# One clock for each engine to place layer one's weight sums and token sums, a tile place lent, staging banks kept

## The chip, the cores and the metric

The kernel runs on one core of one Trainium2 chip. The metric is the device time of the program in microseconds (us), as the median of several runs; the time before is 2650.01 us, with runs from 2649.26 to 2651.77. Where the trace is read, the times are those of one profiled execution of 2648.42 us.

## The reference

Two layers of attention over graphs, on 128 graphs of 64 tokens (32 x 512 x 768 in the inner function is only the shape in which the weights were first made), 768 numbers to a token, in float32. What matters:

```python
h = max(layernorm(x), 0)
for l in range(2):
    u_left  = einsum('bih,bjh->bij', h, h @ W_left[l].T)  / sqrt(768)
    u_right = einsum('bih,bjh->bij', h, h @ W_right[l].T) / sqrt(768)
    u = u_left on and above the diagonal, u_right below it
    e = exp(u) * adj
    attention = e / (e.sum(axis=2) + 1e-10)
    ctx = attention @ (h @ W_lin[l].T + b_lin[l])
    h = relu((ctx - mean) / (std + 1e-3) * ln_a[l] + ln_b[l])
out = x + h
```

The two products with `W_left` and `W_right` are 18 blocks of 256 x 256 on three thirds of the tokens' 768 numbers; the kernel computes them with fewer multiplications by a fixed bilinear scheme.

## The kernel before

Line numbers are those of the kernel before; in the kernel after, the same helper stands 8 lines lower near the top and 84 lower near the end.

**Stages.** For each layer there are a first pass (`pass_one`), which makes the scores and the attention, and a second (`pass_two`), which makes the linear part, the context and the norm. The tokens are cut into 16 batches of 512, numbered 0 to 15, and each batch into two parts of 256. A part is held transposed in a tile `ht` ([128, 6, 256], 768 KB), of which there are six places. In layer one a batch comes to its `ht` by a chain: load x, statistics on VectorE (DVE), the normalisation on ScalarE (ACT), four transposes on DVE into the tile `xb` (one place only, L465), four stores to DRAM (L461), and two loads of `ht` (L368).

**The first pass.** It counts slots, two to a product. Layer one begins with 12 plain blocks (24 matmuls each, slots 0 to 71) for parts 0 and 1; then come ten supers, k = 1 to 10, of three parts each. A super is 40 products (`PRODUCTS`, numbered 0 to 39), each of a weight form with a token form: 8 matmuls of 128 x 256 into one of the banks C, D, X, Y in turn (later also Z and V). Layer two has a super 0 in place of the plain blocks. After product 3 of a super come the scores of the super before (L733, 192 matmuls). ACT and DVE read each bank into the tiles `m` (`reads`, L910, L914, L245); a bank is used again four products later.

**Weight sums.** The weight forms are linear combinations of the 18 raw blocks: 101 sums of two values (`W_OPS`, numbered 18 to 118). Layer one computes them while it runs, in `Weights`: on DVE, or, where the first factor is 1, on GpSimd (POOL). A DVE sum may be staged: ACT first copies one operand into a PSUM bank (Z, V or one of the score banks; L517) and DVE adds from there (L522, L245). The result overwrites an operand that has no other use, or takes one of 51 places `g`. Layer two loads its forms ready made.

**Token sums.** The token forms are 38 sums (`T_OPS`, numbered 9 to 46) of the nine pieces of a super's parts; `Tokens` issues them on POOL (L245), at most 11 of them alive, in places `g`. They are given out one at a time: either ahead, by `tokens.step`, when POOL's clock allows it, or by `tokens.need`, just before the product that uses them.

**The order** is written out by hand and by these clocks; no scheduler changes it. Each engine works through its own queue in that order. `put(slot, f)` plans a step at a slot; `turn_of(slot)` runs the planned steps and then gives out weight sums and token sums, by a clock that is estimated for DVE and POOL:

```python
now = slot * 0.86 if l == 0 or slot >= 80 else slot * 0.6 + 20.8
...
while clock["vector"] <= now and weights.some(nc.vector):
    clock["vector"] += 0.62
...
if clock["pool"] <= now + 1.5 and tokens.step(slot):
    clock["pool"] = max(clock["pool"], now) + 1.35
```

The clock starts at zero in each call of `pass_one`. At the end of the last super of a layer, `final` also plans the second pass's beginnings: the 9 blocks of `W_lin` are loaded, centred on ACT (L233, L237) and combined by 17 sums (`sums_n`, in turn on POOL and DVE), and the first token sums of the second pass go to POOL. The masks `wm` (L745) are POOL's as well.

Of the kernel before, what the change touches and what calls it, by code (L numbers as in the profile page):

```python
# [17 lines left out]
def kernel(  # L18
# [55 lines left out]
            slot += step  # L74
        return slot

    def timed(us, f):
        f.vector = us
        return f

    def run(slot):
        if slot in plan:
# [303 lines left out]
    def transpose_rows(l, u, pool):  # L386

        key, xr, todo = (1, l, u), XR[l, u], []
        if l == 0:
            mv = stat.tile([P, Q, 2], F32, name="mv0", bufs=2)  # L390
            sd = stat.tile([P, Q], F32, name="sd0", bufs=2)
            rs = stat.tile([P, Q], F32, name="rs0", bufs=2)
            nb = stat.tile([P, Q], F32, name="nb0", bufs=2)

            def scale(q0, q1):
                def deviation():
                    nc.scalar.activation(sd[:, q0:q1], mv[:, q0:q1, 1], AF.Sqrt, bias=eps_in)

                def inverse():
                    nc.vector.reciprocal(rs[:, q0:q1], sd[:, q0:q1])  # L400
                    if q1 - q0 == 1:

                        nc.vector.tensor_scalar(nb[:, q0:q1], mv[:, q0:q1, 0], rs[:, q0:q1], -1.0,
                                                op0=ALU.mult, op1=ALU.mult)
                        return
                    nc.vector.scalar_tensor_tensor(nb[:, q0:q1], mv[:, q0:q1, 0], -1.0, rs[:, q0:q1],
                                                   op0=ALU.mult, op1=ALU.mult)
# [6 lines left out]
            stats = [timed(1.2, lambda q=q: mean_var(mv[:, q, :], [xr[q][:, :HH], xr[q][:, HH:]])) for q in range(Q)]  # L414
            norms = [lambda q=q: norm(q) for q in range(Q)]
            if u:
                for f in stats + [lambda: [f() for f in scale(0, Q)]] + norms:
                    todo.extend([f, None])
            else:

                dev, inv = zip(*(scale(q, q + 1) for q in range(Q)))
                todo.extend([stats[START[0]], dev[START[0]]])
                for q, after in zip(START, START[1:] + (None,)):
                    if after is not None:
                        todo.append(stats[after])
                    todo.append(inv[q])
                    if after is not None:
                        todo.append(dev[after])
                    if q == START[2]:

                        todo.append(lambda: turn(0, START[0]))
                    todo.append(norms[q])
# [29 lines left out]
                                  xb[a * 32:(a + 1) * 32].rearrange("i (c b) q j -> i c b (q j)", b=4))  # L462

        for q in range(Q):
            todo.append(timed(0.9, lambda q=q: nc.vector.transpose(  # L465
                xb[:, :, q, :], xr[q].rearrange("p (b j) -> p b j", j=32))))
            todo.append(None)
        todo.append(store)
        return todo
# [1 line left out]
    def places(pool, shapes, names):  # L471
        for n in names:
            shape, bufs = shapes[n]
            pool.tile(shape, F32, name=n, bufs=bufs)

    class Weights:
        def __init__(self, ops, plain, stay, extra=()):
            self.at, self.left, self.stay = {}, list(ops), stay  # L480
            self.uses = {}
            for _, a, _, b, _ in W_OPS:
                for v in (a, b):
                    self.uses[v] = self.uses.get(v, 0) + 1
            for v in range(18):
                self.uses[v] = self.uses.get(v, 0) + plain
            for f in FORMS:
                self.uses[f] = self.uses.get(f, 0) + 1
            self.stage = []
            self.mine = {id(t) for t in extra}  # L490
            self.extra = deque(extra)

        def used(self, v):
            self.uses[v] -= 1
# [4 lines left out]
        def take(self):  # L499
            of = max(self.extra, free, key=len)  # L500
            return of.popleft() if of else None

        def emit(self, eng, op):
            v, a, ca, b, cb = op
            x, y = self.at[a], self.at[b]
            dead = next((s for s in (a, b) if self.uses[s] == 1 and not (self.mine and s >= 18)), None)
            t = self.take() if dead is None else self.at[dead]
            if t is None:
                return False
            if dead is not None:  # L510
                self.uses[dead] = 0
                del self.at[dead]
            if self.stage and eng is nc.vector:
                bank = self.stage.pop(0)
                self.stage.append(bank)
                bank = bank.rearrange("p (c d) -> p c d", c=K2)
                nc.scalar.copy(bank, x)  # L517
                x = bank
            if ca == 1:
                added(eng, t, "+" if cb > 0 else "-", x, y)  # L520
            else:
# [6 lines left out]
            self.left.remove(op)  # L528
            return True

        def some(self, eng, reach=10):
            for op in self.left[:reach]:
                if op[1] in self.at and op[3] in self.at and (eng is nc.vector or op[2] == 1):
                    if eng is nc.vector and op[2] == 1 and any(o[2] != 1 and o[1] in self.at and o[3] in self.at
                                                               for o in self.left[:reach // 2]):
                        continue
                    return self.emit(eng, op)
            return False

        def need(self, v):  # L540
            if v not in self.at:
                op = next(o for o in self.left if o[0] == v)
                self.need(op[1])
                self.need(op[3])
                assert self.emit(nc.vector, op)
            return self.at[v]


# [34 lines left out]
    class Tokens:  # L583
        LIMIT = 11

        def __init__(self, l):
# [4 lines left out]
                self.uses[v] = self.uses.get(v, 0) + 1  # L591
            self.count = {}


        def value(self, k, v, cut=False):
            if v >= 9:
# [11 lines left out]
                    for p in SUPER[0]]  # L608

        def step(self, slot, eng=None):  # L610
            if self.k >= len(SUPER) or slot < self.ready.get(self.k, 10 ** 9) or self.out >= self.LIMIT or not free:
# [17 lines left out]
        def used(self, k, v):  # L629
            n = self.count[k, v] = self.count.get((k, v), 0) + 1  # L630
            if v >= 9 and n == self.uses[v]:
                free.append(self.at.pop((k, v)))
                self.out -= 1

        def need(self, k, v):
# [2 lines left out]
            return self.value(k, v)  # L638


    SPACE = (((0, 46, 97), (-12, 34, 97)), ((10, 46, 97), (10, 46, 97)))

    TOKENS, fetch = [Tokens(l) for l in range(L)], deque()
# [11 lines left out]
    def pass_one(l, start, final):  # L655
        with tc.tile_pool(name=f"one{l}", bufs=2, reuse_waits="tile") as sp, \
# [170 lines left out]
            if l:  # L827
                weights.uses.update({f: 1 for f in FORMS})
            weights.at = W[l, "raw"]
            clock = {"pool": 0.0, "vector": 0.0}  # L830

            def turn_of(slot):
                now = slot * 0.86 if l == 0 or slot >= 80 else slot * 0.6 + 20.8
                clock["vector"] = max(clock["vector"], now - 1.0) + sum(getattr(f, "vector", 0.0) for f in plan.get(slot, ()))
                run(slot)
                if fetch and slot >= start["weights"] and slot % 3 and free:
                    fetch.popleft()()
                if weights.left and slot >= start["weights"]:
                    while clock["vector"] <= now and weights.some(nc.vector):
                        clock["vector"] += 0.62  # L840
                    if clock["pool"] <= now and start["pool"] <= slot < start["tokens"]:
                        if weights.some(nc.gpsimd, 40):
                            clock["pool"] = max(clock["pool"], now) + 1.35
                if clock["pool"] <= now + 1.5 and tokens.step(slot):
                    clock["pool"] = max(clock["pool"], now) + 1.35


            follow = {}

            def prepare(b, slot, step=1):  # L850
# [5 lines left out]
                for t in range(2):  # L856
# [7 lines left out]
                    put(at, lambda p=p, hold=before >= 0: load_part(1, l, p, hold))  # L864
# [14 lines left out]
            for n, (w, t) in enumerate(order):  # L879
                bank = bank_of(n % CHAINS)  # L880
                for j in range(3):
# [3 lines left out]
                    if j == 2:  # L885
                        if n == 0 and mid:
                            mid()
                            weights.stage = [KEEP["Z"], KEEP["V"], KEEP["scores"][:, 0]]
                        nc.scalar.copy(into(6 * t + w), out_of(bank))
                    turn_of(slot + 1)  # L890
                    slot += 2
            weights.stage = []

            last = len(SUPER) - 1
            for k in range(FIRST_OF[l], len(SUPER)):
# [8 lines left out]
                def reads(i):  # L904
                    for o, c in READS[i]:
                        bank = out_of(bank_of(CHAINS * (k - 1) + i % CHAINS), k == 0, o)
                        to = into(o, k == 0)
                        if o not in seen:
                            seen.add(o)
                            nc.scalar.activation(to, bank, AF.Copy, scale=float(c))  # L910
# [454 lines left out]
```

## Time and profile before

| what | value |
|---|---|
| median of 3 runs | 2650.01 us (2649.26 to 2651.77) |
| profiled execution | 2648.42 us, its span 2646.6 us |
| mean granted TensorE clock | 0.995 |
| busy: PE / DVE / POOL / ACT | 98% / 67% / 67% / 35% of the span |
| DMA | 331.84 MB, 125 GB/s |

The span is counted from the first to the last instruction. A row of a timeline gives the start and the length of a group of like instructions on one engine, the line, the operation, the tiles written and read, shapes and count, and in brackets the idle time ahead of it and what ended that. A row of the busy time by stage gives a window, its length, each engine's busy time with the count of instructions, then the granted clock of TensorE (1.00 is full), the DMA engines' share and their rate.

### The profile page before, as it was taken

The page shows a single profiled execution, that of the slowest core. Times are in us where ns is not written, and L with a number is a line of the kernel's source. Part 1 is how long each engine was busy: PE and PEld are TensorE (multiplying, and loading weights), DVE is VectorE, ACT ScalarE, POOL GpSimd, SP SyncE. Part 2 cuts the span into 40 slices and gives each one's busy share as a digit, 9 for nine tenths or more (in the row PEclk, how much of TensorE's full clock was granted, in tenths as well). Part 3 has the DMA queues.
Part 4 walks back from the last instruction along what each step waited for, and adds up shares of the span by engine and source line. Part 5 has one row for each costly group of instructions (what it writes and reads, how often), then busy time and mean ns, then how long its engine had stood idle before and what let it go on. Part 6 is the DMA issues. An engine that isn't in the chain of part 4 may idle for free. (4 is left out here: it accounts for less than half of the span.)

```text
span 2646.6 us, 47202 instructions
## 1 busy us (share of the span) xinstructions
PE 2591.6 (98%) x18122; PEld 2217.1 (84%) x18122; DVE 1780.6 (67%) x2888; ACT 935.4 (35%) x1969; POOL 1763.1 (67%) x1392
## 2 busy tenths in 40 slices
PE   9899999999999999999999999999999989999998
PEld 8788888888888888888798888888888878887886
DVE  7878787777768445554456667677666676666667
ACT  5522223223113244454542222122222335555453
POOL 4766676666668657676276666667666657878786
PEclk9999999999999999999999999999999999999999
DMA  7443534343421354445794424253532215555655
GB/s 220 113 111 86 124 93 110 93 119 79 98 60 56 123 156 149 159 139 182 219 282 101 121 68 108 71 129 93 136 98 70 67 49 157 157 167 166 177 161 146
DMA packets 258465, 331.84 MB, mean 125 GB/s; under 512 B 56002, under 2 KB 190402, under 8 KB 258242
## 3 DMA queue, kind: packets, MB, share of 16 engines
q1 hardware_dynamic: 241442, 320.56, 44.3%
q10 hardware_dynamic: 16800, 8.26, 1.2%
q8 instruction: 145, 2.38, 0.4%
q14 instruction: 78, 0.64, 0.1%
HBM read 213.39 MB, written 115.34 MB: 124 GB/s over the span
## 5 line engine op out<-in xcount | busy, mean ns | idle before, releaser
L245 POOL TENSOR_TENSOR g<-ht 128x512 f32<-128x512 f32 (+1 forms) x620 | 785.9, 1279 | 420.8 <-PE Z L702 71.6
L245 POOL TENSOR_TENSOR g<-g,g 128x512 f32<-128x512 f32 (+1 forms) x310 | 397.9, 1291 | 136.7 <-PE C L702 22.0
L245 POOL TENSOR_TENSOR g<-ht,g 128x512 f32<-128x512 f32 (+1 forms) x272 | 346.1, 1282 | 164.8 <-PE Z L702 42.8
L702 PE MATMUL X<-g,g 128*128 128x256 f32 (+1 forms) x1080 | 252.9, 377 | 6.0 <-DVE m L914 6.0
L1006 PE MATMUL Z<-g,g 128*128 128x256 f32 x1024 | 244.1, 380 | 3.5 <-ACT hl L300 3.2
L702 PE MATMUL C<-g,g 128*128 128x256 f32 x1008 | 239.7, 381 | 4.9 <-POOL g L245 2.2
L702 PEld LDWEIGHTS X<-g,g 128*128 128x128 f32 x1080 | 203.0, 191 | 34.8 <-DVE m L914 6.8
L702 PE MATMUL Y<-g,g 128*128 128x256 f32 (+1 forms) x968 | 225.7, 376 | 3.8 <-POOL g L245 3.8
L1006 PEld LDWEIGHTS Z<-g,g 128*128 128x128 f32 x1024 | 191.6, 190 | 35.8 <-issue 4.1
L379 ACT ACTIVATE ht<-ht,b_col,a_col 128x256 f32<-128x256 f32 x384 | 196.1, 591 | 69.0 <-DMA ht<-h 53.8
L702 PEld LDWEIGHTS C<-g,g 128*128 128x128 f32 x1008 | 190.5, 190 | 32.9 <-POOL g L245 3.5
L702 PE MATMUL Z<-g,g 128*128 128x256 f32 (+1 forms) x936 | 217.0, 375 | 0.0
L702 PE MATMUL D<-g,g 128*128 128x256 f32 x880 | 209.8, 381 | 1.8 <-POOL g L245 1.8
L702 PEld LDWEIGHTS Y<-g,g 128*128 128x128 f32 x968 | 182.0, 190 | 27.8 <-POOL g L245 4.2
L702 PE MATMUL V<-g,g 128*128 128x256 f32 (+1 forms) x840 | 194.6, 375 | 3.1 <-POOL g L245 1.6
L702 PEld LDWEIGHTS Z<-g,g 128*128 128x128 f32 x936 | 174.5, 190 | 23.1
L702 PEld LDWEIGHTS D<-g,g 128*128 128x128 f32 x880 | 168.1, 191 | 25.7 <-POOL g L245 2.5
L1006 PE MATMUL X<-g,g 128*128 128x256 f32 x768 | 182.7, 379 | 0.0
L702 PEld LDWEIGHTS V<-g,g 128*128 128x128 f32 x840 | 157.6, 191 | 23.3 <-POOL g L245 1.7
L1206 POOL TENSOR_TENSOR z<-z,b 128x768 f32<-128x768 f32 x62 | 112.7, 1829 | 81.7 <-DVE z L1203 77.2
L245 DVE TENSOR_TENSOR m<-m,Y 128x512 f32<-128x512 f32 (+2 forms) x196 | 126.5, 667 | 58.4 <-ACT m L910 35.7
L245 DVE TENSOR_TENSOR m<-m,D 128x512 f32<-128x512 f32 x180 | 118.2, 677 | 70.0 <-ACT m L910 51.3
(222 smaller groups left out, 4612.0 us busy)
## 6 DMA issues: line engine op xcount, KB each, us to landing
ht<-h SPq DMA_DIRECT2D x126, 768.0 KB, 6.3
h<-xb SPq DMA_DIRECT2D x124, 384.0 KB, 6.6
z<-z SPq DMA_DIRECT2D x128, 192.0 KB, 3.1
x<-z SPq DMA_DIRECT2D x128, 192.0 KB, 5.4
xr<-in_x_dram SPq DMA_DIRECT2D x120, 192.0 KB, 3.8
out_dram<-xr SPq DMA_DIRECT2D x120, 192.0 KB, 2.7
x<-in_x_dram SPq DMA_DIRECT2D x112, 192.0 KB, 5.4
g<-form SPq DMA_DIRECT2D x40, 256.0 KB, 5.6
```

The lines of the kernel that those rows point to most:

```text
L245: (eng.tensor_add if sign == "+" else eng.tensor_sub)(o, a, b)
L379: nc.scalar.activation(ht, ht, AF.Relu, bias=cols[1][:, c:c + 1], scale=cols[0][:, c:c + 1])
L702: nc.tensor.matmul(o, w[:, c, g * P:(g + 1) * P], t, start=(new and g == c == at == 0), stop=(c == K2 - 1), skip_group_check=True)
L1006: nc.tensor.matmul(p[:, n], b[t][:, c, r * P:(r + 1) * P], w[s][:, c, :], start=(i in FIRST and i not in PRELOAD and n == c == 0), stop=(c ...
L1206: nc.gpsimd.tensor_add(zs[k], zs[k], rows["b"])
```

## The change

The clock now has an entry for DVE, ACT and POOL, is defined once for the kernel, and is set only when layer one begins. `timed` names an engine and a duration for a planned step, and `turn_of` adds these. `Weights.begins` estimates when a sum could start, from when its operands are made (`made`), when the place it writes is last read (`until`), and when the staging bank is free; `some` takes the sum that could start first and gives it out only if that is within 3 us. One place `g` is kept spare once token sums have begun, and `Tokens` may hold two fewer while weight sums are left. The banks Z and V stay staging banks during the supers of layer one. Part 5's tile `ht` is named early and three pieces of it are lent to token sums that are used up before product 20 (`own`, `SOON`); its load moves from slot 49 to slot 113, in super 1. The batches 1 and 2 are prepared from slots 19 and 31 instead of 16 and 30. In layer one the last weight sum is given out at slot 113 instead of 76.

The diff, cut to its core:

```diff
+    clock = {"vector": 0.0, "scalar": 0.0, "pool": 0.0}
...
     def load_part(which, l, p, hold=False):
-        ht = HT[which, l, p] = big.tile([P, C, TH], F32, name="ht", bufs=6)
+        if (which, l, p) not in HT:
+            HT[which, l, p] = big.tile([P, C, TH], F32, name="ht", bufs=6)
+        ht = HT[which, l, p]
...
+        def begins(self, eng, op):
+            dead = self.dead(op)
+            t = self.at[dead] if dead is not None else (self.extra or free or (None,))[0]
+            x, y = (self.made.get(s, 0) for s in (op[1], op[3]))
+            at = max(y, self.until.get(id(t), 0), clock[NAMES[eng]])
+            if self.stage and eng is nc.vector:
+                x = max(x, clock["scalar"], self.until.get(id(self.stage[0]), 0)) + 0.6
+            return max(x, at)
...
         def emit(self, eng, op):
...
+            if dead is None and len(free) <= self.spare:
+                return False
...
+            us = 1.3 if eng is nc.gpsimd or not self.stage else 0.65
+            end = clock[NAMES[eng]] = self.made[v] = at + us
...
-        def some(self, eng, reach=10):
-            for op in self.left[:reach]:
...
+        def some(self, eng, reach, now):
+            ops = [(max(self.begins(eng, op), now) + (0.4 if eng is nc.vector and op[2] == 1 else 0), n, op)
+                   for n, op in enumerate(self.left[:reach])
+                   if op[1] in self.at and op[3] in self.at and (eng is nc.vector or op[2] == 1)
+                   and (len(free) > self.spare or self.dead(op) is not None)]
+            if not ops:
+                return False
+            at, _, op = min(ops)
+            return at <= now + 3 and self.emit(eng, op)
...
-            t = free.popleft()
+            t = (self.own if self.own and self.last[v] < SOON else free).popleft()
...
-            clock = {"pool": 0.0, "vector": 0.0}
-
+            if not l:
+                clock.update(vector=3.0, scalar=0.0, pool=3.0)
+                weights.made.update({b: max(0.0, 0.52 * b - 1.4) if b < 9 else 3.9 + 0.9 * (b - 9) for b in range(18)})
             def turn_of(slot):
-                now = slot * 0.86 if l == 0 or slot >= 80 else slot * 0.6 + 20.8
-                clock["vector"] = max(clock["vector"], now - 1.0) + sum(getattr(f, "vector", 0.0) for f in plan.get(slot, ()))
+                now = slot * 0.87 if l == 0 or slot >= 80 else slot * 0.6 + 20.8
+                if slot == start["tokens"]:
+                    weights.spare = 1
+                for e in clock:
+                    clock[e] = max(clock[e], now - 0.5)
+                for f in plan.get(slot, ()):
+                    passes(f)
                 run(slot)
...
-                    while clock["vector"] <= now and weights.some(nc.vector):
-                        clock["vector"] += 0.62
-                    if clock["pool"] <= now and start["pool"] <= slot < start["tokens"]:
-                        if weights.some(nc.gpsimd, 40):
-                            clock["pool"] = max(clock["pool"], now) + 1.35
+                    while clock["vector"] <= now + (2 if slot > 2 * PLAIN else 0.5) and weights.some(nc.vector, 10, now):
+                        pass
+                    if slot < start["tokens"]:
+                        while clock["pool"] <= now + 0.5 and weights.some(nc.gpsimd, 40, now):
+                            pass
+                tokens.limit = Tokens.LIMIT - 2 * bool(weights.left)
                 if clock["pool"] <= now + 1.5 and tokens.step(slot):
                     clock["pool"] = max(clock["pool"], now) + 1.35
...
+                tokens.own.extend(HT[1, 0, 5][:, j * K2:(j + 1) * K2, :] for j in range(3))
...
+                def back():
+                    assert len(tokens.own) == 3
+                    tokens.own.clear()
+                    load_part(1, 0, 5)
+
+                put(begins(1) + 2 * SOON + 1, back)
...
-            weights.stage = []
+            weights.stage = [] if l else [KEEP["Z"], KEEP["V"]]
...
-    pass_one(0, {"weights": 0, "pool": 8, "tokens": 60, 1: 16, 2: 30}, final_of(0))
+    pass_one(0, {"weights": 0, "tokens": 60, 1: 19, 2: 31}, final_of(0))
```

More of the change, by code (lines that the diff above doesn't have):

```diff
@@ L75, in put_all, with timed, passes @@
         return slot
-    def timed(us, f):
-        f.vector = us
-        return f
+    clock = {"vector": 0.0, "scalar": 0.0, "pool": 0.0}
+    def timed(f, *steps):
+        f.steps = steps
+        return f
+    def passes(f):
+        for e, us in getattr(f, "steps", ()):
+            clock[e] += us
     def run(slot):
@@ L412, in norm, with waits @@
                 nc.scalar.activation(xr[q], xr[q], AF.Relu, bias=nb[:, q:q + 1], scale=rs[:, q:q + 1])
[L414 to L415 removed]
+            stats = [timed(lambda q=q: mean_var(mv[:, q, :], [xr[q][:, :HH], xr[q][:, HH:]]), ("vector", 1.2))
+                     for q in range(Q)]
+            norms = [timed(lambda q=q: norm(q), ("scalar", 1.0)) for q in range(Q)]
             if u:
[L417 removed]
+                deviation, inverse = scale(0, Q)
+                def waits():
+                    clock["scalar"] = max(clock["scalar"], clock["vector"]) + 0.4
+                    clock["vector"] = max(clock["vector"], clock["scalar"]) + 0.5
+                    deviation()
+                    inverse()
+                for f in stats + [waits] + norms:
                     todo.extend([f, None])
@@ L491, in __init__ @@
             self.extra = deque(extra)
+            self.made, self.until, self.spare = {}, {}, 0
         def used(self, v):
@@ L501, in take, with dead @@
             return of.popleft() if of else None
+        def dead(self, op):
+            return next((s for s in (op[1], op[3]) if self.uses[s] == 1 and not (self.mine and s >= 18)), None)
+        def begins(self, eng, op):
[6 more added lines that the diff above has]
+            return max(x, at)
         def emit(self, eng, op):
@@ L505, in emit @@
             x, y = self.at[a], self.at[b]
-            dead = next((s for s in (a, b) if self.uses[s] == 1 and not (self.mine and s >= 18)), None)
+            dead, at = self.dead(op), self.begins(eng, op)
+            if dead is None and len(free) <= self.spare:
+                return False
             t = self.take() if dead is None else self.at[dead]
@@ L509, in emit @@
                 return False
+            us = 1.3 if eng is nc.gpsimd or not self.stage else 0.65
+            end = clock[NAMES[eng]] = self.made[v] = at + us
+            if self.stage and eng is nc.vector:
+                bank = self.stage.pop(0)
+                self.stage.append(bank)
+                clock["scalar"] = max(self.made.get(a, 0), clock["scalar"], self.until.get(id(bank), 0)) + 0.6
+                self.until[id(bank)] = end
+                bank = bank.rearrange("p (c d) -> p c d", c=K2)
+                nc.scalar.copy(bank, x)
+                x = bank
+            for s in (a, b):
+                self.until[id(self.at[s])] = max(self.until.get(id(self.at[s]), 0), end)
+            self.until[id(t)] = end
             if dead is not None:
@@ L512, in emit @@
                 del self.at[dead]
[L513 to L518, printed above, removed]
             if ca == 1:
@@ L592, in __init__ @@
             self.count = {}
+            first = {t: i for i, (_, t) in reversed(list(enumerate(PRODUCTS)))}
+            for v, a, b, _ in reversed(T_OPS):
+                for s in (a, b):
+                    first[s] = min(first.get(s, 99), first[v])
+            self.last = {v: max([i for i, (_, t) in enumerate(PRODUCTS) if t == v] +
+                                [first[o] for o, *ab, _ in T_OPS if v in ab]) for v, *_ in T_OPS}
+            self.own, self.mine, self.limit = deque(), set(), self.LIMIT
         def value(self, k, v, cut=False):
@@ L610, in step @@
         def step(self, slot, eng=None):
-            if self.k >= len(SUPER) or slot < self.ready.get(self.k, 10 ** 9) or self.out >= self.LIMIT or not free:
+            if self.k >= len(SUPER) or slot < self.ready.get(self.k, 10 ** 9) or self.out >= self.limit or not free:
                 return False
@@ L631, in used @@
             if v >= 9 and n == self.uses[v]:
-                free.append(self.at.pop((k, v)))
+                t = self.at.pop((k, v))
+                (self.own if id(t) in self.mine else free).append(t)
                 self.out -= 1
```

25 lines of the change are left out of this document (16 added, 9 removed).

## The prediction

> **What bounds the kernel now.** The page's first part comes first.
>
> ```profile
> PE 2591.6 (98%) x18122; PEld 2217.1 (84%) x18122; DVE 1780.6 (67%) x2888; ACT 935.4 (35%) x1969; POOL 1763.1 (67%) x1392
> ```
>
> TensorE is busy for all but 55 us of the span (2646.6 us), and the sum of its matmuls is untouched by the change. So the change is worth what it does to TensorE's gaps. Where they are is read from the busy time by stage, and the largest from TensorE's timeline:
>
> ```profile
> 74.70:99.50 24.80, 15.98 (x226) 12.53 (x225) 20.64 (x36) 14.65 (x27) 19.14 (x16) 0.79 0.50 127
> 99.50:130.00 30.50, 30.50 (x141) 26.77 (x142) 24.37 (x45) 12.73 (x21) 22.26 (x19) 1.00 0.33 72
> ```
>
> ```profile
> 69.55 5.34 PE L702 MATMUL Y<-ht,g 128*128 128x256 f32 x24
> 77.08 2.51 PE L702 MATMUL C<-g,g 128*128 128x256 f32 x8 [2.19 <-POOL g L245]
> 81.39 3.78 PE L702 MATMUL D<-g,g 128*128 128x256 f32 x8 [1.79 <-POOL g L245]
> ...
> 90.80 2.57 PE L702 MATMUL Y<-g,g 128*128 128x256 f32 x8 [3.80 <-POOL g L245]
> 93.30 5.16 PE L733 MATMUL sc<-m,ht 128*32 128x95 f32 x192
> 99.49 1.97 PE L702 MATMUL C<-g,g 128*128 128x256 f32 x8 [1.04 <-ACT m L910]
> ...
> 120.29 1.89 PE L702 MATMUL C<-g,g 128*128 128x256 f32 x8
> ...
> 125.47 1.89 PE L702 MATMUL Y<-g,g 128*128 128x256 f32 x8
> ```
>
> Columns after the range of the first fence: length, then busy time (and instructions) of PE, PEld, DVE, ACT, POOL, then granted clock. TensorE is idle for 8.8 us of the 24.8 us in which layer one passes from the plain blocks to super 1, and never in the 30 us behind it. Products 0 to 3 each wait for a token sum of GpSimd (POOL g); product 4 starts at 99.49. Product 16 starts at 120.29 and product 19 at 125.47: 1.727 us apart, the pitch where nothing waits. The lost time is not all idle: products 1 to 3 and the scores also run at half clock.
>
> ```profile
> 78.30:85.20 6.90, 5.11 (x13) 0.51 1.04 233
> 92.30:95.70 3.40, 3.40 (x71) 0.53 0.01 2
> ```
>
> ```profile
> 837.23 1.99 PE L702 MATMUL X<-g,g 128*128 128x256 f32 x8 [2.90 <-DVE m L914]
> ```
>
> The first two rows are the busy time by stage of PE alone: 0.51 and 0.53 is the granted clock behind the gaps of 2.19, 1.79 and 3.80 us. After the one of 2.90 us at 837.23 the product took 1.99 us, so the clock was not halved there. I price a gap over 3 us at one halved stretch of about 3.4 us (the 92.30 row), some 1.7 to 2 us of extra time. [...]
>
> **Part A: the hole at 74.7 to 99.5 goes.** Why the token sums are late is in DVE's, SP's and POOL's timelines:
>
> ```profile
> 44.37 3.54 DVE L465 STREAM_TRANSPOSE xb<-x 128x768 f32<-128x768 f32 x4
> 61.05 3.55 DVE L465 STREAM_TRANSPOSE xb<-m 128x768 f32<-128x768 f32 x4
> 65.69 0.68 DVE L245 TENSOR_TENSOR g<-sc,g 128x512 f32<-128x512 f32 x1
> 66.28 0.68 DVE L245 TENSOR_TENSOR g<-Z,g 128x512 f32<-128x512 f32 x1
> ```
>
> ```profile
> 47.94 5.23 SPq L461 DMA_DIRECT2D h<-xb  x4
> 64.62 5.17 SPq L461 DMA_DIRECT2D h<-xb  x4
> ```
>
> ```profile
> h<-xb SPq DMA_DIRECT2D x8, 384.0 KB, 7.2
> ```
>
> ```profile
> 44.53 9.90 POOL L245 TENSOR_TENSOR g<-g,g 128x512 f32<-128x512 f32 x8 [8.91 <-DVE g L522]
> ...
> 78.72 1.27 POOL L245 TENSOR_TENSOR g<-ht 128x512 f32<-128x512 f32 x1 [0.45 <-DMA ht<-h]
> ...
> 83.09 2.51 POOL L245 TENSOR_TENSOR g<-ht 128x512 f32<-128x512 f32 x2 [1.75 <-DVE g L522]
> ```
>
> POOL's first token sums follow weight sums that wait for DVE, and two of them the load of the second batch's tokens: transposed from 61.05, stored from 64.62, loaded and used at 78.72, 14.1 us behind the first store. A weight sum on DVE costs 0.60 us (65.69 to 66.28), a sum on POOL 1.24 us (9.90 / 8).
>
> After the change DVE does fewer weight sums early. The first batch's transposes come out of its order to end at 42.3 instead of 47.9, and the stores leave at once. They take as long as before: the last of four is issued 3.9 us behind the first (5.23 x 3/4) and lands 7.2 us later, so all are in at 42.4 + 11.1 = 53.5. The second batch's transposes write the same tile xb, and now no weight sum stands between the two: DVE waits from 47.6 to 53.5, a wait that was covered before. It does them to 57.0, and the weight sum queued behind them to 57.4. The first stores are off at 57.1, hence this batch's tokens usable at 57.1 + 14.1 = 71.2 instead of 78.7. POOL, which waits for that weight sum, goes on with nine of its own to 57.4 + 9 x 1.24 = 68.6 and token sums from there. That gives 70 us for product 0's sum (needed at 74.73, the end of the last plain block), 73.9 and 75.1 for those of products 1 and 2 (needed at 76.5 and 78.2) and 79.6 for product 3's (needed at 79.9; it overwrites what product 1 reads until 78.2). So nothing waits, by margins of 4.7, 2.6, 3.1 and 0.3 us. The scores follow at 74.73 + 4 x 1.727 = 81.64 for 5.16, then 1.04 for the read of C: product 4 at 87.84 instead of 99.49, a gain of 11.6 us, at full clock. If the margins break it is 0.3 to 3 us less.
>
> **Part B: what is late next.** Ten weight sums of DVE that were finished before the hole now stand in super 1 up to product 16, mixed with its bank reads, and four behind it. In the order of the changed kernel, weight sum 115 is the last of the ten; token sum 34 on POOL writes over what it reads and waits for it, 35 waits for 34, and product 19 needs 35.
>
> ```profile
> 103.19 0.55 DVE L406 SCALAR_TENSOR_TENSOR nb<-mv,rs 128x4 f32<-128x4 f32 x1
> ...
> 122.74 0.69 DVE L914 SCALAR_TENSOR_TENSOR m<-C,m 128x512 f32<-128x512 f32 x1
> ...
> 123.34 0.68 DVE L914 SCALAR_TENSOR_TENSOR m<-C,m 128x512 f32<-128x512 f32 x1
> ```
>
> ```profile
> 103.74:124.62 20.88, 17.50 (x33) 1.00 0.23 45
> ```
>
> Counted in the time of before (everything from product 4 on moves as a block by part A): behind nb (ends 103.74) DVE has 17.5 us of work up to the end of product 16's reads at 124.62, with 3.4 us of idle. Nine of the ten sums fall into it, 9 x 0.60 = 5.4 us, more than that idle. Serially that is 103.74 + 17.5 + 5.4 = 126.6; the staged sums also wait for ScalarE's copies, which stand in its queue behind bank reads, about 1.5 us as in the gaps between such sums before. Sum 115 ends at 128.2, token sums 34 and 35 at 130.9, and product 19 starts 5.4 us late. At best, with sum 115 straight behind the read of 123.34 (ends 124.02), it is 124.7 + 2.6 = 127.3, 1.8 us late; at worst, with none of DVE's idle recovered, 3.4 us more than my value, 8.8. Then token sum 37 takes the place of 36, which product 20 reads: product 21 waits for one POOL sum and its handover, 1.45 us, whatever the clock does. One halved stretch behind a 5 us gap: 1.8 (0 to 3.4). Part B: +8.7 (3.3 to 13.6).
>
> The lent place costs nothing itself: part 5's load, 768 KB, leaves at slot 113 instead of 49; its first use is 40 slots on, 34 us, against some 14 us from store to use above. The staging banks kept through super 1 are what gives 0.60 us to the late weight sums; no product writes them there. A plus B: -11.6 + 8.7 + 0.3 = -2.6.
>
> **Part C: layer two, by the kept clock.** The clock is set back only for layer one. In layer two POOL's still stands at the end of layer one's count, near 758 us, and the test that lets a token sum be given out ahead fails until slot 870. So every token sum of layer two is given out only when its product needs it. In supers 0 to 9 the leads in POOL's order stay three products or more, and I price that at 0. In the last super POOL also has the sums of the output weights (8 of them) and the first token sums of the second pass. Before, the last token sums had been given out ahead of these; now they stand behind.
>
> ```profile
> 2121.96 1.27 POOL L245 TENSOR_TENSOR g<-g,g 128x512 f32<-128x512 f32 x1 [3.37 <-ACT g L968]
> ...
> 2127.81 1.27 POOL L245 TENSOR_TENSOR g<-g,g 128x512 f32<-128x512 f32 x1 [2.11 <-ACT g L237]
> ...
> 2139.64 1.28 POOL L245 TENSOR_TENSOR g<-g,g 128x512 f32<-128x512 f32 x1 [1.94 <-DVE g L245]
> 2140.88 1.73 POOL L245 TENSOR_TENSOR g<-ht 128x512 f32<-128x512 f32 x1
> ```
>
> ```profile
> 2121.62 1.89 PE L702 MATMUL Y<-g,g 128*128 128x256 f32 x8
> ...
> 2125.07 1.89 PE L702 MATMUL D<-g,g 128*128 128x256 f32 x8
> ...
> 2137.22 3.38 PE L702 MATMUL X<-g,g 128*128 128x256 f32 x8 [3.10 <-DVE m L914]
> ...
> 2142.17 1.89 PE L702 MATMUL C<-g,g 128*128 128x256 f32 x8
> ```
>
> Product 23 (2121.62) needs token sum 39, now behind the sum that starts at 2121.96: it ends at 2124.5, a wait of 2.9 us. Product 25 (2125.07, then 2128.0) needs one behind the sum of 2127.81: 2130.4, a wait of 2.4. Product 26 then 0.8. These 6.1 us partly fill the old gap of 3.10 us ahead of product 30 and its halved clock (3.38 against 1.89). Token sum 44, for product 32, stands behind the sum of 2139.64, which waits for a DVE sum that itself stands behind bank reads and so moves about 2 us later: five POOL operations of 1.28 to 1.73 us from 2142 on, then one more, end at 2150 to 2151. Product 32, at 2142.17 before, is thus 8 to 9 us late, product 33 another 0.9. With one halved stretch (+1.7) and 1 to 2 us taken up by gaps that come later, part C is +9.5; if DVE's sum does not move, +6, and with a second halved stretch, +13.
>
> **Sum.** -2.6 + 9.5 = +6.9 on the profiled 2648.42 gives 2655.3. The median of the runs stood 1.6 above the profiled one, so the forecast is 2657.0.
>
> **Rivals.** (1) Part C does not bite, since POOL's sums wait there for events that come earlier than I think: then A and B alone, 2650.0 - 2.6 = 2647.4. For it: TensorE already idles there, so some of the delay is free; against it: the rows of 2121.96 and 2139.64 show the very waits. (2) The planner's estimates are right and DVE keeps up in super 1, and POOL in layer two: only A and the 1.45 us, 2640. For it: DVE is idle for 20% of 99.5 to 130; against it: that idle is less than the ten sums. (3) It goes further to the slow side: lateness feeds itself where product 19 waits, because DVE's and ScalarE's bank reads, the copies and POOL's reuse all stand in line behind one another, so the wait at product 19 is 8.8 us and each later token sum starts with no lead. It decides where sum 115 ends later than 130. With part C at 13: 2665. Since I forecast slower, rival 2 is the other side.
>
> **How the numbers follow.** What a measurement here can tell from no change is about 0.2%, 5.3 us. My own sum has 0.54: from the bounds of B and C it spans 2649 to 2665, two parts in three of it over 2655.3. Rival 1 has 0.20, rival 2 0.09, rival 3 0.17. Faster by over 0.2% (under 2644.7): rival 2 and a small part of rival 1, 0.12. Slower: 0.43 of my own and rival 3, 0.60. The rest, 0.28, is same. The range 2646 to 2665 leaves out rival 2 and the ends of 1 and 3.
>
> **What would show it.** In the profile after: no wait for POOL ahead of products 0 to 3, the scores near 81.6 and product 4 near 88; DVE waiting for the stores ahead of the second transposes near 48 to 53; a wait of about 5 us for POOL ahead of product 19 and about 1.4 ahead of product 21, with a halved clock behind; in the last super of layer two waits for POOL at products 23, 25 and 32 in place of the one for DVE at product 30. Wrong I would be first if product 19 waits for less than 2 us, or if layer two's span is as before.

## The result, and the profile after

The changed kernel takes 2664.06 us (2662.11 to 2666.3) against 2650.76 for the kernel before: ratio 1.0049, 95% interval 1.0033 to 1.0064, so 13.3 us slower. Its profiled execution took 2662.11 us with a span of 2660.3, 13.7 more than the profiled execution before; the shares below go by these two.

The busy time by stage (columns as before: length, PE, PEld, DVE, ACT, POOL, clock, DMA):

```profile
74.70:99.50 24.80, 20.67 (x267) 17.36 (x266) 15.63 (x33) 15.20 (x28) 20.51 (x18) 1.00 0.21 45
99.50:130.00 30.50, 24.23 (x96) 19.55 (x95) 24.91 (x43) 11.03 (x19) 13.61 (x11) 0.89 0.35 78
```

The hole has shrunk from 8.8 us of idle at a clock of 0.79 to 4.1 at full clock, and the stage behind it, which had been full, is now idle for 6.3 us. TensorE's timeline of the kernel after shows where:

```profile
74.81 1.89 PE L760 MATMUL C<-ht,g 128*128 128x256 f32 x8
78.36 1.99 PE L760 MATMUL D<-ht,g 128*128 128x256 f32 x8 [1.66 <-POOL ht L253]
80.19 1.89 PE L760 MATMUL X<-g,g 128*128 128x256 f32 x8
83.52 1.99 PE L760 MATMUL Y<-ht,g 128*128 128x256 f32 x8 [1.44 <-POOL ht L253]
85.44 4.13 PE L791 MATMUL sc<-m,ht 128*32 128x95 f32 x192
90.60 1.96 PE L760 MATMUL C<-g,g 128*128 128x256 f32 x8 [1.03 <-ACT m L994]
...
115.89 1.97 PE L760 MATMUL X<-ht,g 128*128 128x256 f32 x8 [0.31 <-DVE m L253]
123.73 3.78 PE L760 MATMUL Y<-ht,g 128*128 128x256 f32 x8 [5.87 <-POOL ht L253]
127.30 2.96 PE L760 MATMUL C<-g,g 128*128 128x256 f32 x8
131.73 1.99 PE L760 MATMUL D<-g,g 128*128 128x256 f32 x8 [1.47 <-POOL g L253]
133.78 1.99 PE L760 MATMUL X<-g,g 128*128 128x256 f32 x8
```

Product 4 starts at 90.60 instead of 99.49. Product 19 (123.73) then waits 5.87 us, runs with product 20 at half clock, and product 21 waits 1.47. Product 22 starts at 133.78; in the kernel before it was here:

```profile
130.65 1.89 PE L702 MATMUL X<-g,g 128*128 128x256 f32 x8
```

So 8.9 us gained at product 4 have turned into 3.1 lost eighteen products later, and at product 22 of layer two's last super 2.7 of them are still there (2122.60 for 2119.89). There the rest goes (TensorE, then POOL, of the kernel after):

```profile
2127.54 1.99 PE L760 MATMUL Y<-g,g 128*128 128x256 f32 x8 [3.06 <-POOL g L253]
...
2133.88 1.99 PE L760 MATMUL D<-g,g 128*128 128x256 f32 x8 [2.62 <-POOL g L253]
2136.33 1.99 PE L760 MATMUL X<-g,g 128*128 128x256 f32 x8 [0.46 <-POOL g L253]
...
2153.38 3.75 PE L760 MATMUL C<-g,g 128*128 128x256 f32 x8 [6.43 <-POOL g L253]
```

```profile
2125.00 2.49 POOL L253 TENSOR_TENSOR g<-g,g 128x512 f32<-128x512 f32 x2 [4.59 <-DVE g L253]
...
2130.89 1.27 POOL L253 TENSOR_TENSOR g<-g,g 128x512 f32<-128x512 f32 x1 [2.17 <-ACT g L245]
2132.11 1.72 POOL L253 TENSOR_TENSOR g<-ht,g 128x512 f32<-128x512 f32 x1
...
2143.37 1.28 POOL L253 TENSOR_TENSOR g<-g,g 128x512 f32<-128x512 f32 x1 [1.94 <-DVE g L253]
```

Products 23, 25, 26 and 32 wait for token sums that stand in POOL's queue behind the output weights' sums, and these wait for DVE and ACT. POOL itself was idle for 4.59, 2.17 and 1.94 us ahead of them: it is the order that costs, not POOL's work.

### The profile page after: what moved, and what is told of

Its sections match the earlier page's. It is cut to its first block, busy times and chain, and to the rows that moved or that the text cites. A ratio compares the mean times of both kernels' runs of the same rounds, so it can differ in the third digit from the quotient of the medians.

```text
span 2660.3 us, 47199 instructions
## 1 busy us (share of the span) xinstructions
PE 2591.8 (97%) x18122; PEld 2214.3 (83%) x18122; DVE 1778.8 (67%) x2876; ACT 933.2 (35%) x1965; POOL 1777.3 (67%) x1404
## 5 line engine op out<-in xcount | busy, mean ns | idle before, releaser
L760 PE MATMUL X<-g,g 128*128 128x256 f32 (+1 forms) x1056 | 247.5, 377 | 4.9 <-DVE m L998 4.4
L760 PE MATMUL Y<-g,g 128*128 128x256 f32 (+1 forms) x928 | 215.7, 375 | 3.1 <-POOL g L253 3.1
L760 PE MATMUL D<-g,g 128*128 128x256 f32 x856 | 202.5, 379 | 4.1 <-POOL g L253 4.1
L760 PEld LDWEIGHTS Y<-g,g 128*128 128x128 f32 x928 | 173.9, 190 | 26.3 <-POOL g L253 3.9
L760 PEld LDWEIGHTS D<-g,g 128*128 128x128 f32 x856 | 162.3, 190 | 27.4 <-POOL g L253 5.0
```

The costliest lines, as they stand in the source:

```text
L760: nc.tensor.matmul(o, w[:, c, g * P:(g + 1) * P], t, start=(new and g == c == at == 0), stop=(c == K2 - 1), skip_group_check=True)
```

## The experiments

They ran in three groups, each on a chip of its own: e1 to e4, e5 to e8, e9 to e11. The kernel before took 2653.6, 2653.9 and 2653.3 us there (medians). What counts is each one's ratio to it, and where two experiments are set against each other it is by these ratios.

**e1: is layer two's loss the clock that was not set back?**

```diff
             if not l:
                 clock.update(vector=3.0, scalar=0.0, pool=3.0)
                 ...
+            else:
+                clock.update(vector=0.0, scalar=0.0, pool=0.0)
```

> The changed kernel with the clock set back to zero in layer two as well; nothing else differs. My theory: the loss of 10.5 us in layer two comes from the clock that still stands at layer one's end, so the waits for POOL at products 23, 25 and 32 of the last super (3.06, 2.62 and 6.43 us) go, the wait for DVE at product 30 (3.1 us) comes back, layer one is as in the changed kernel (p19 waits 5.9 us), and the time is 2664 - 10.5 = 2653.5, some 3 us over the kernel before. Rival: layer two is late because it starts out of step with its loads and DVE after layer one; then the waits stay and the time is 2662 to 2666.

2654.45 us, ratio 1.0003 (0.9995 to 1.0012): the change without the stale clock can't be told from the kernel before; the 3 us that were expected over it lie just inside the interval. Layer one's waits stayed (5.87 us at product 19) and the last super looks as before, with one wait for DVE at product 30:

```profile
123.35 3.78 PE L760 MATMUL Y<-ht,g 128*128 128x256 f32 x8 [5.87 <-POOL ht L253]
...
2143.68 2.00 PE L760 MATMUL X<-g,g 128*128 128x256 f32 x8 [3.09 <-DVE m L1000]
```

Between the ratios 1.0049 and 1.0003 lie 12 us. The traces put 10.7 into the last super: in the changed kernel product 22 is 2.7 us later than in the kernel before, and the start of the second pass behind that super 13.4 (2188.38 for 2174.97).

**e2: and does that clock alone do it?**

```diff
-            clock = {"pool": 0.0, "vector": 0.0}
+            clock = {"pool": 758.0 if l else 0.0, "vector": 0.0}
```

> The kernel before with one number changed: POOL's clock starts layer two at 758 instead of 0. My theory: this alone brings the waits of the last super of layer two, 2650.8 + 10.5 = 2661, with layer one as before (four gaps of 2.19, 1.79, 3.80 and 1.04 us). Rival: without the rest of the change it costs nothing, 2650.8.

2667.74 us, ratio 1.0055 (1.0042 to 1.0068), 14.6 us over the kernel before, where 10.5 were expected. In the trace products 23, 25, 26 and 32 of the last super wait for POOL, as in the changed kernel:

```profile
2130.43 3.58 PE L702 MATMUL Y<-g,g 128*128 128x256 f32 x8 [3.07 <-POOL g L245]
2136.28 1.99 PE L702 MATMUL D<-g,g 128*128 128x256 f32 x8 [0.53 <-POOL g L245]
2139.78 1.99 PE L702 MATMUL X<-g,g 128*128 128x256 f32 x8 [1.51 <-POOL g L245]
2156.33 3.78 PE L702 MATMUL C<-g,g 128*128 128x256 f32 x8 [5.92 <-POOL g L245]
```

From product 22 to the start of the second pass this kernel loses 10.9 us against the kernel before (5.6 late, then 16.5). The 5.6 us ahead of that are no work of this edit: 5.4 of them arise in layer one, whose code it leaves as it was, and no run says why.

e1 and e2 together show it both ways: take the stale clock away and the loss goes, add it alone and the loss comes.

**e3: is product 19's wait the place of the weight sums in DVE's queue?** One bound, on top of e1:

```diff
-                    while clock["vector"] <= now + (2 if slot > 2 * PLAIN else 0.5) and weights.some(nc.vector, 10, now):
+                    while clock["vector"] <= now + 2 and weights.some(nc.vector, 10, now):
```

> As e1_clock_reset, and DVE's weight sums are given out up to 2 us ahead of the clock in the plain blocks too (0.5 in the changed kernel), so that sum 115 is given out at slot 76 instead of 106 and the last at 88 instead of 113. My theory: product 19's wait (5.9 us), the wait at product 21 (1.5) and the halved clock behind them (3) come from the place of these sums in DVE's queue; they go, and the time is 2653.5 - 10 = 2643.5, or up to 3 us more where the token sums of products 1 to 3 now start behind more sums. Rival: the wait at product 19 comes from too few places g for token sums, so it stays with 4 us or more: 2652.

2645.99 us, ratio 0.9969 (0.9957 to 0.9981): 8.2 us under the kernel before, 9 under e1. Product 19 waits for nothing, nor does product 21. The wait at product 1 is smaller too, and POOL's timeline names its cause, the load of the second batch's tokens (TensorE, then POOL, of e3):

```profile
77.20 1.99 PE L760 MATMUL D<-ht,g 128*128 128x256 f32 x8 [0.68 <-POOL ht L253]
...
82.37 1.99 PE L760 MATMUL Y<-ht,g 128*128 128x256 f32 x8 [1.44 <-POOL ht L253]
...
89.45 1.97 PE L760 MATMUL C<-g,g 128*128 128x256 f32 x8 [1.03 <-ACT m L996]
```

```profile
74.53 1.27 POOL L253 TENSOR_TENSOR g<-ht 128x512 f32<-128x512 f32 x1 [4.21 <-DMA ht<-h]
```

The rival, too few places, falls: with the sums given out early the token sums come early by themselves.

**e4: would DVE do better with sums in place of its wait for the first stores?** e3 with `2: 37` instead of `2: 31`.

> As e3_sums_early, and the second batch is prepared from slot 37 instead of 31, so that five weight sums of DVE stand between the two batches' transposes where DVE waited 5.5 us for the stores. My theory: that wait shrinks to about 2.5 us, the sums behind it and POOL's start 3 us earlier, so the waits at products 1 and 3 (1.66 and 1.44 us) go and the time is 1.5 to 3 us under e3_sums_early. Rival: the stores, not DVE, set when the second batch's tokens come, so nothing is gained: the same as e3_sums_early, or up to 2 us slower since the transposes come later.

2650.7 us, ratio 0.9988 (0.998 to 0.9997), about 5 us worse than e3 by the ratios, more than either side had said. DVE's wait fell from 5.2 to 2.35 us as expected, and it did not help: the second batch's stores left at 61.09 instead of 59.08, and POOL waited 8.53 us for its tokens. Product 1 waited 2.25 us (e3: 0.68), and products 6, 7 and 9, which wait for nothing in e3, 1.47, 1.47 and 1.10. My theory fell; the chain of the stores is what counts, as the rival had it, at a higher price.

**e5: the second batch transposed into a place of its own** (on top of e3; the tiles of parts 4 and 5 serve in place of `xb`):

```diff
+        if (l, u) == (0, 2):
+            hs = [HT[1, 0, p].rearrange("p c t -> p (c t)") for p in (4, 5)]
+            ...
+            for q in range(Q):
+                for s, h in enumerate(hs):
+                    ... nc.vector.transpose(h of q, xr[q], blocks 2s and 2s + 1 of each four)
```

> As e3_sums_early, but the second batch is transposed into the two ht tiles of parts 4 and 5, which are empty then, instead of into xb: eight half transposes and eight half stores of the same data. My theory: what is left of the hole in e3 (0.68 us at product 1, 1.44 at product 3) comes from one chain, first batch's stores landed, second batch's transposes, its stores, its load; DVE's wait of 5.2 us for the first stores goes, the second batch's tokens come 4 to 5 us earlier, both waits go, and product 4 starts at 87.9 instead of 89.45: 1.5 to 2.5 us under e3. Rival: POOL's own weight sums, or the stores queueing in the DMA engines, set the token sums, and the waits stay: the same as e3.

2650.89 us, ratio 0.9986 (0.9976 to 0.9997), some 4.5 us over e3 by the ratios, whose intervals overlap a little, with executions from 2643 to 2656. The profiled one did not test the theory, as DVE's and POOL's timelines of e5 show (POOL's row has the part of its run that lies in the window asked for):

```profile
50.19 7.99 DVE L416 SCALAR_TENSOR_TENSOR nb<-mv,rs 128x4 f32<-128x4 f32 x1
59.28 1.04 DVE L487 STREAM_TRANSPOSE ht<-m 128x384 f32<-128x384 f32 x2 [1.09 <-ACT m L422]
```

```profile
39.71 18.46 POOL L253 TENSOR_TENSOR g<-g,g 128x512 f32<-128x512 f32 x15
```

An instruction on four numbers a partition took 8 us, and ended where POOL's run of sums did (39.71 + 18.46 = 58.17; 50.19 + 7.99 = 58.18).

**e6: without the lent place.**

> As e3_sums_early without the lent place: no piece of part 5's tile is given to token sums, and part 5 is loaded at the slot that it had in the kernel before. My theory: the lent place costs nothing and, with the weight sums early, brings little: token sums are given out at most 2 or 3 slots later, and the time is within 2 us of e3. Rival: three places fewer hold the token sums of products 1 to 20 back, and waits for POOL of 3 us or more come back in super 1.

2649.55 us, ratio 0.9985 (0.9976 to 0.9994), 4 us over e3 by the ratios, whose intervals overlap a little; my 2 us were probably too few, and the rival's waits of 3 us did not come. Waits for POOL of 1.93 us at product 3 and 2.00 at product 7 show that three places fewer do hold the first token sums back: product 15 starts at 114.13, in e3 at 108.90. The two profiled executions as a whole lie only 0.4 us apart.

**e7: the batches from slots 16 and 30, as in the kernel before** (on top of e3).

> As e3_sums_early with the batches prepared from slots 16 and 30, as in the kernel before, instead of 19 and 31: three weight sums fewer stand ahead of the first batch's statistics on DVE. My theory: the first batch's transposes end up to 1.5 us earlier (its rows arrive at 34.1, so no more than that), all of the chain to the second batch's tokens with them, and products 1 and 3 wait for 1 us less in sum: 1 us under e3. Rival: the transposes wait for the normalisation on ScalarE and nothing moves: the same as e3.

2643.93 us, ratio 0.9958 (0.9946 to 0.9971). The first batch's transposes ended at 42.4 instead of 44.4, POOL had the second batch's tokens at 73.84, product 1 waits for nothing and product 3 for 1.34. The gain over e3 is 3 us by the ratios, and their intervals overlap.

**e8: no staging in super 1** (`weights.stage = []`, on top of e3).

> As e3_sums_early, but no staging after the plain blocks: the six or seven weight sums of super 1 read both operands from the tiles g. My theory: such a sum takes up to 1.8 us where POOL runs beside it, against 0.68 staged, but DVE has 6 us of idle between 85 and 91, which take it up: within 1.5 us of e3. Rival: the sums are now on the path (sum 115 is used by token sum 34, and bank reads stand behind them): 3 us or more over e3.

2647.28 us, ratio 0.9978 (0.9969 to 0.9988), 2.4 us over e3 with intervals that overlap: not decided by the times. Of the sums that it changes, some took 0.68 to 0.80 us and one 1.77. Its profiled execution had the stall of e5 as well, in its rows of DVE and POOL:

```profile
49.86 8.00 DVE L416 SCALAR_TENSOR_TENSOR nb<-mv,rs 128x4 f32<-128x4 f32 x1
```

```profile
43.07 14.77 POOL L253 TENSOR_TENSOR g<-g,g 128x512 f32<-128x512 f32 x12
```

**e9: nb without two tile operands** (on top of e7):

```diff
-                    nc.vector.scalar_tensor_tensor(nb[:, q0:q1], mv[:, q0:q1, 0], -1.0, rs[:, q0:q1],
-                                                   op0=ALU.mult, op1=ALU.mult)
+                    for q in range(q0, q1):
+                        nc.vector.tensor_scalar(nb[:, q:q + 1], mv[:, q:q + 1, 0], rs[:, q:q + 1], -1.0,
+                                                op0=ALU.mult, op1=ALU.mult)
```

> As e7_first_batch_sooner, but nb (four numbers a partition) comes by four instructions with rs as a per-partition scalar instead of one that reads mv and rs as two tiles. In e5 and e8 that one instruction took 8.0 us at 50 us, to the end of POOL's run of sums, and held the second batch back; in e3 and e7 0.65. My theory: DVE's read of two tiles waited for POOL; without it no nb takes over 0.3 us, and the time is as e7, 2643, or 1 us less, with none of the slow executions of 2650 and more that e5, e6 and e8 had. Rival: the 8 us are something else on DVE, and they turn up on the four instructions too.

2641.5 us (2638.62 to 2644.38), ratio 0.996 (0.9946 to 0.9974): by the median the fastest, 10.6 us under the kernel before, and not to be told from e7. None of the fifteen executions of e9 to e11 reached 2650, but neither did the five of e7, so the times do not show that this stall made the long executions of e5, e6 and e8. The four instructions take 0.58 us together:

```profile
47.01 0.58 DVE L417 TENSOR_SCALAR nb<-mv,rs 128x1 f32<-128x1 f32 x4
```

**e10 and e11: the second place again, with nb by scalar**; e11 with the batches from 16 and 29.

> As e5_second_place with nb by scalar as in e9. e5 had the 8.0 us in its profiled execution, so it did not test the second place. My theory, as for e5: DVE's wait for the first batch's stores (5.2 us) goes, the second batch's tokens come 4 us earlier than in e3, products 1 and 3 wait for nothing, product 4 starts at 87.9: 2643. Rival: the waits at products 1 and 3 stay over 1 us in sum, since POOL's weight sums or the stores set them: 2646.

> e10 with the batches prepared from slots 16 and 29. My theory: with the second place the first batch no longer matters to the second, so this brings nothing over e10 but what comes from the order of the weight sums: within 1.5 us of e10 and of e9. Rival: the earlier second batch puts its statistics ahead of weight sums that POOL's sums wait for, and product 0 or 1 waits for POOL by 1 us or more.

2643.59 us, ratio 0.9967 (0.9954 to 0.9979), and 2644.04, ratio 0.9965 (0.9951 to 0.9979). Now the mechanism shows: DVE no longer waits for the stores, POOL has the tokens at 71.56 (e3: 74.53), product 1 waits for nothing, product 4 starts at 88.09. But a wait is left at product 3, the same in both (TensorE, then POOL, of e10):

```profile
78.03 1.89 PE L780 MATMUL X<-g,g 128*128 128x256 f32 x8
81.01 1.99 PE L780 MATMUL Y<-g,g 128*128 128x256 f32 x8 [1.10 <-POOL g L253]
```

```profile
78.33 1.27 POOL L253 TENSOR_TENSOR ht<-ht,g 128x512 f32<-128x512 f32 x1 [1.68 <-PE D L780]
79.69 1.27 POOL L253 TENSOR_TENSOR g<-ht 128x512 f32<-128x512 f32 x1
```

Two token sums follow one another after product 1 has let go of a place, and product 3 needs the second: no earlier load can help. e11 tests it, for there the tokens came at 68.48, 3 us earlier than in e10, and product 3 waited 1.09 us. What e10 wins at product 1 it gives back behind product 4, with waits of 1.47, 1.47 and 0.52 us at products 6, 7 and 11.

## Why the prediction was right, and where it was off

The forecast was +6.9 us on the profiled execution; +13.7 came, and the time lies 0.9 us inside the upper end of the range. The hole shrank, product 19 became late and layer two's last super lost time, all at the places that were named; the waits at products 1 and 3 were not forecast. Each of the three sizes erred to the same side.

**Part A** was put at -11.6 us and measured -8.9 (99.49 to 90.60). The step that failed is "the first batch's transposes come out of its order to end at 42.3". A weight sum ahead of them waited for ScalarE's copy, which ran behind two of the four normalisations (38.37 to 40.32):

```profile
40.83 0.69 DVE L566 SCALAR_TENSOR_TENSOR g<-Z,g 128x512 f32<-128x512 f32 x1 [2.50 <-ACT Z L555]
41.44 3.55 DVE L484 STREAM_TRANSPOSE xb<-x 128x768 f32<-128x768 f32 x4
...
56.00 3.56 DVE L484 STREAM_TRANSPOSE xb<-m 128x768 f32<-128x768 f32 x4 [5.54 <-DMA h<-xb]
```

They ended at 44.99, and nearly all of the 2.7 us went down the chain: second transposes at 56.0 for 53.5, the second stores off at 59.6 for 57.1. From there to the first use of these tokens I had carried over 14.1 us; it took 16.1. The load was issued as long behind the first store as before (6.35 us), but landed 9.6 us after that, where 7.7 had been enough from issue to use (SP, then POOL, of the kernel after):

```profile
59.59 5.16 SPq L480 DMA_DIRECT2D h<-xb  x4
65.94 0.87 SPq L378 DMA_DIRECT2D ht<-h  x1
66.85 9.02 SPq L369 DMA_DIRECT2D x<-in_x_dram  x8
```

```profile
75.68 1.28 POOL L253 TENSOR_TENSOR g<-ht 128x512 f32<-128x512 f32 x1 [1.83 <-DVE g L253]
```

The row names a DVE sum that ended at 75.58; the load had landed at 75.5, so either would have held POOL. Eight loads of x now follow this load after 0.9 us, where they followed after 5 us before; whether they slowed it, no run shows. Late by 4.5 us in all against a margin of 2.6, product 1 waited 1.66. The 0.3 us at product 3 were never there: of two sums behind product 1's end I had counted one, and e10 shows 1.1 us that remain. Two readings of the rows were off as well. The 5.16 us for the scores were read from a row at half clock; at full clock they took 4.13, 1.0 us to the good. And of products 0 to 3 only 0, 1 and 3 had waited in the kernel before; its row of product 2 names no wait. The new wait for the stores came as said: 5.9 us forecast for DVE before the second transposes, 5.54 measured.

**Part B** was put at +8.7 and measured +12.0. From product 4 to 18 the changed kernel loses 1.0 us in small waits, which I had left out. Product 18 to 19 takes 7.84 us for 1.73, a loss of 6.1 for 5.4, because weight sum 115 ends 30.3 us behind product 4's start and not 28.7:

```profile
120.23 0.68 DVE L566 SCALAR_TENSOR_TENSOR g<-V,g 128x512 f32<-128x512 f32 x1
```

```profile
121.06 1.27 POOL L253 TENSOR_TENSOR g<-ht,g 128x512 f32<-128x512 f32 x1 [7.39 <-DVE g L566]
122.41 1.27 POOL L253 TENSOR_TENSOR ht<-ht,g 128x512 f32<-128x512 f32 x1
```

The wait at product 21 was right (1.45 forecast, 1.47). The halved clock was mis-sized: one stretch of 3.4 us was priced, two came, some 3.1 us for 1.8 (the clock of TensorE by window):

```profile
122.60:129.40 6.80, 5.67 (x13) 0.50 0.27 66
```

The 0 at the low end of that price, behind a gap of 5 us, no run shows: behind the waits of 5.87, 5.92 and 6.43 us the products took 3.75 to 3.78 us for 1.89.

**Part C** was put at +9.5 and comes to 10.7, from product 22's 2.7 us late to the second pass's 13.4. Products 23, 25 and 26 wait for 3.06, 2.62 and 0.46 us, forecast 2.9, 2.4 and 0.8; product 32 starts 11.2 us late, 8.5 more than the shift of 2.7 (forecast 8 to 9), and the old wait at product 30 is filled as said. Product 33's 0.9 us did not come. e1 and e2 confirm the cause.

**The rivals.** The first, that part C does not bite, is refuted. The second, that the planner's estimates hold, failed at both places that it named. The third gave 2665, where the result is, but not by its mechanism: product 19 waited 5.87 us and not 8.8, and part C was 10.7 and not 13. In the chances, two parts in three of 0.54 are 0.36 and not the 0.43 that went into "slower". **The lent place**, costed at nothing, seems to pay once the rest is repaired: 4 us by the two ratios, whose intervals overlap a little, and 5.2 us up to product 15 in the traces of e3 and e6. That staging gives the late sums their 0.60 us is left open by e8.

## What to carry to other kernels

An order that is planned by an estimated clock is a program of its own: read where each step lands in every engine's queue, in every later use of the clock too, and not only in the stage that it was written for. When sums are made lazier, ask what stands behind them in the queue at the new place; here one bound, 2 instead of 0.5 us ahead, turned the change from no gain into 8 us. When a margin in a chain of transposes, stores and loads is as thin as the 2.6 us here, where the tokens came 4.5 us late, carry a late first step through to the end before the gain is counted.

## What the runs showed of the hardware

A DVE instruction that reads two small tiles lasted through some six GpSimd sums in two profiled executions. nb, 128 x 4, took 8.0 us in e5 and e8, to the end of a run of back-to-back sums on POOL (58.18 beside 58.17 in e5, 57.86 beside 57.84 in e8), and 0.66 us in e3 beside such a run:

```profile
49.65 0.66 DVE L416 SCALAR_TENSOR_TENSOR nb<-mv,rs 128x4 f32<-128x4 f32 x1
```

```profile
42.85 14.82 POOL L253 TENSOR_TENSOR g<-g,g 128x512 f32<-128x512 f32 x12
```

A sum of that run took 1.23 us in e5 (18.46 / 15). That nb's read of two tiles waited there for POOL is my reading of where it ended; what held it, no run shows. The scalar form never took long: of the 180 such instructions in the profiled executions of e9 to e11 none took over 0.22 us, while the 150 of the other form in the ten executions before them took from 0.16 to 8.0, all but the two shown at most 1.24. What decides when 8 us come, no run shows. Nor do they explain every long execution: the profiled one of e4, the longest of its twelve (2656.52), had no nb over 1.22.

The halving of the clock is not decided by the length of a wait alone. The same wait at product 23 of the last super lasted 3.06 us in the changed kernel and 3.07 in e2; behind the first the product took 1.99 us, behind the second 3.58. A wait of 1.59 us in the kernel before, ahead of 1351.17, was followed by 3.4 us at a clock of 0.57; one of 3.23 us in the kernel after, ahead of 1394.27, by 3.4 us at 1.00. My threshold of 3 us was a reading of too few rows. The waits of 5.87, 5.92 and 6.43 us were all halved. What else decides it, no run shows.
